# The first loads of a two-layer gated network: weights and first row in halves, other queues, fewer filler matmuls

## The chip, the core and the metric

The kernel runs on one core of a Trainium2 chip. A core has a matrix engine (TensorE, PE in the profile; its weight loads are shown apart as PEld), a vector engine (VectorE, DVE), an activation engine (ScalarE, ACT), GpSimd (POOL) and SyncE (SP), which issues transfers. ACT issues transfers too. Transfers move data from the chip's memory into the on-chip buffers and run on 16 DMA engines. The metric is the device time of one execution in microseconds (us), less being better; the time given is the median of several runs.

## The reference

x is 8 sequences of 128 tokens with 512 features, so 1024 tokens. Two layers follow one another, each a conditioning step and a gated feed-forward network with a residual:

```
base = x @ W.T                                   # 512 x 512
logits = x @ Wr.T + 5 * onehot(token id)         # 8 experts
gates = softmax over the best two logits
cond = base + 2 * sum_e gates[e] * (x @ A[e].T) @ B[e].T       # rank 16 each
x = x + down0(silu(gate0(cond)) * up0(cond))     # 4-bit weights, 1376 wide
c = x @ w1[adapter id].T                         # one matrix per sequence
x = x + down1(silu(gate1(norm(c))) * up1(norm(c)))   # 1792 wide
```

Of this the change touches the loads for the first step: `Wr` and `A` (together `WA`, 136 columns), the token ids that lie behind them, and x.

## The kernel before, in words

Features lie on the 128 partitions in 4 chunks (`KC`), tokens along the rows. Float32 products in the large matmuls are split into a high and a low part and added up in three passes (`base_products`, i = 0, 1, 2), so much of the time of ACT and VectorE goes into making these parts.

The stage at issue is the start. Here is what each line does:

- L220 loads `wa`: the expert weights `WA` and the ids, one transfer of 276 KB on SP's queue.
- L221 to L224 load x as `xb`, one transfer of 256 KB for each of the 8 sequences ("rows"). The even rows are issued by ACT, the odd ones by SP.
- L225 to L230 load W in four pieces (`wT`), B (`bT`) and a small table; all on SP. Behind them SP issues the quantised weights, their zeros and the residual.
- L243 to L246: VectorE writes a square of ones, and TensorE multiplies it by itself `NWARM` = 37 times into a bank that nobody reads.
- L287, `experts(tb)`: for each row of a half of the tokens (`tb` 0: rows 0 to 3, `tb` 1: rows 4 to 7), four accumulating matmuls over the chunks `c`, of `xb[:, row, c]` with `wa[:, c]`. A float32 matmul appears in the profile as two instructions, so a row is 8.
- L306, `gated(tb, ...)`: VectorE finds the best two experts, ACT takes one exponential (`ex`, L325) in between, VectorE weighs the low-rank products (`hg`).
- L357 to L384 make the split parts of x and of W: `x_high` and `w_high` on ACT (L359, L377), `x_scaled` on ACT (L369), `x_low`, `x_diff`, `w_low`, `w_diff` on VectorE.
- L387, `base_products`, and L414, `low_rank` (L416), add up the base and the low-rank term in PSUM; L670 and L671 (`split_condition`, on ACT and VectorE) turn the sum into the parts `a` that the first layer's gate and up matmuls (L539) read.

The order of PE, DVE and ACT in this stage is written out by hand from L697 on: `experts(0)`, the parts of rows 0 to 3, `experts(1)`, two pieces of `w_high`, `gated(0)`, the other two pieces, the parts of rows 4 to 7, and then the base products. Each engine works through its own list in that order and waits on semaphores of the others. Transfers are issued in the order of the program on each queue. PSUM tiles are pairs of banks from one pool of four.

Of the kernel before, what the change touches and what calls it, by code (L numbers as in the profile page):

```python
# [23 lines left out]
B, T, D = 8, 128, 512  # L24
NT = B * T
TB = 512
NTB = NT // TB
NWARM = 37
KC = D // P
E, R = 8, 16  # L30
LANG_BIAS = 5.0
# [57 lines left out]
def network(tc: tile.TileContext, a, out, by_groups, flag=None, again=None):  # L89


    with ExitStack() as ctx:
        network_in(ctx, tc, a, out, by_groups, flag, again)


def network_in(ctx, tc, a, out, by_groups, flag, again):
    nc = tc.nc
# [7 lines left out]
    def bank(name):  # L105
        return pair(name)[:, 0, :]
# [104 lines left out]
    xb = cp.tile([P, B, KC, T], F32, name="xb")  # L211
# [4 lines left out]
    wa_ids = cp.tile([P, KC * (E + E * R) + COND_PLACE], I32, name="wa")[:, : KC * (E + E * R) + B]  # L216
    wa = wa_ids[:, : KC * (E + E * R)].bitcast(F32).rearrange("p (c n) -> p c n", c=KC)
    ids0 = wa_ids[:, KC * (E + E * R) :]

    nc.sync.dma_start(out=wa_ids, in_=a["WA"])  # L220
    for b in range(B):  # L221
        (nc.scalar, nc.sync)[b % 2].dma_start(
            out=xb[:, b].rearrange("p c t -> p (c t)"), in_=a["xb"][b]
        )  # L224
    for m in range(KC):  # L225
        nc.sync.dma_start(out=wT[:, m, :], in_=a["WT"][:, m, :])
    nc.sync.dma_start(out=bT, in_=a["BT"])
# [16 lines left out]
    idle = bank("idle")[:, :P]  # L244
    for _ in range(NWARM):
        nc.tensor.matmul(idle, lhsT=ones, rhs=ones, start=True, stop=True)  # L246
# [1129 lines left out]
```

## Time and profile before

| what | value |
|---|---|
| median of 3 runs | 436.3 us (435.57 to 436.6) |
| the profiled execution | 436.83 us, span 434.9 us |
| mean granted clock of TensorE | 0.996 |
| base matmuls, L390, starting at | 12.90 us |
| first gate matmuls of layer 0, L539 | 43.16 us in the chain |
| `xb` on ACT's queue, 4 transfers of 256 KB | median 5.6 us from issue to landing |
| `xb` on SP's queue, 4 transfers of 256 KB | median 6.1 us |
| `wa`, 276 KB on SP's queue | 3.6 us |
| `wT`, 4 pieces of 256 KB on SP's queue | median 5.9 us |

The span runs from the first to the last instruction of the program; the execution's time also holds what lies around it. A row of the timeline has the start, the length, the engine, the line, the operation, the tiles written and read, and, in brackets, how long the engine stood idle before it and what ended that. "SPq" and "ACTq" are the sequencers that issue transfers. A busy TensorE is not TensorE at its peak, since its matmuls overlap.

### The profile page before, as it was taken

Reading aid. Unit: us, or ns where it says so; the run is one execution under the profiler, and the core shown is the slowest. Engines: PE = TensorE matmul, PEld = TensorE weight load, DVE = VectorE, ACT = ScalarE, POOL = GpSimd, SP = SyncE. Lnnn points to the kernel's source line nnn. Section 1 sums busy time; section 2 is a strip of 40 time slices with the busy share of each in tenths; the row PEclk is TensorE's granted clock in tenths of the full one; section 3 lists DMA queues with packets and bytes.
Section 4 is the critical chain, followed back from the end, with each engine's and each line's share of the span. In section 5 each row is a group of like instructions: output and inputs, shape, how many; then the busy total and the mean of one; then the engine's idle time right before and its main releaser. Section 6 shows DMA issues by size and latency. Waiting matters only on the chain.

```text
span 434.9 us, 4847 instructions
## 1 busy us (share of the span) xinstructions
PE 424.8 (98%) x1855; PEld 334.5 (77%) x1855; DVE 302.4 (70%) x432; ACT 232.0 (53%) x269; POOL 9.0 (2%) x20
## 2 busy tenths in 40 slices
PE   8999999999999999999999999999999999999992
PEld 8875778888888764447888888888888888888882
DVE  3998979998998769768179634679334676725552
ACT  5923899678877765347478132484132471425420
POOL 1000000000002001100000000000000000000000
PEclk9999999999999999999999999999999999999998
DMA  8931301010001505842114101132001110000013
GB/s 290 344 150 49 98 0 50 18 37 2 0 2 48 242 6 204 301 167 83 64 50 145 48 2 48 50 97 72 2 0 48 50 48 26 0 0 2 2 53 146
DMA packets 12094, 33.07 MB, mean 76 GB/s; under 512 B 1568, under 2 KB 4256, under 8 KB 11040
## 3 DMA queue, kind: packets, MB, share of 16 engines
q1 hardware_dynamic: 9760, 22.21, 15.3%
q0 software_dynamic: 1152, 8.39, 5.1%
q10 hardware_dynamic: 1152, 2.10, 1.3%
q8 instruction: 16, 0.26, 0.2%
q14 instruction: 14, 0.11, 0.1%
HBM read 30.59 MB, written 2.10 MB: 75 GB/s over the span
## 4 chain that ended last, share of the span: by engine, by line
PE 91%; DVE 4%; DMA 2%; ACT 1%; issue 0%; SPq 0%; ACTq 0%; DVEq 0%
PE gate L1056 18%; PE up L1056 18%; PE down L1121 17%; PE gate L539 9%; PE down L587 8%; PE up L539 8%; PE base L390 5%; PE adapt L999 5%; PE base L416 2%; DMA xb<-in_xb 2%; PE experts L293 1%; DVE xT L599 1%; PE nxT L1019 1%; ACT sl L555 1%; DVE h L558 1%; DVE w L952 1%
## 5 line engine op out<-in xcount | busy, mean ns | idle before, releaser
L1056 PE MATMUL gate<-a,w 128*128 128x512 f32 x336 | 81.8, 390 | 0.0
L1056 PE MATMUL up<-a,w 128*128 128x512 f32 x336 | 81.4, 389 | 0.0
L1121 PE MATMUL down<-h,d 128*128 128x512 f32 x336 | 76.8, 389 | 0.0
L1056 PEld LDWEIGHTS up<-a,w 128*128 128x128 f32 x336 | 63.1, 188 | 13.2
L1121 PEld LDWEIGHTS down<-h,d 128*128 128x128 f32 x336 | 63.1, 188 | 13.1
L1056 PEld LDWEIGHTS gate<-a,w 128*128 128x128 f32 x336 | 62.7, 188 | 13.5 <-ACT gate L179 0.6
L1073 DVE SCALAR_TENSOR_TENSOR h<-up,sl 128x1024 f32<-128x1024 f32 (+1 forms) x16 | 17.5, 1092 | 51.0 <-PE up L1056 44.6
L539 PE MATMUL gate<-a,dq 128*128 128x512 f32 (+1 forms) x176 | 47.7, 393 | 0.1
L539 PE MATMUL up<-a,dq 128*128 128x512 f32 (+1 forms) x176 | 47.4, 391 | 0.0
L587 PE MATMUL down<-h,wd 128*128 128x512 f32 (+1 forms) x176 | 42.3, 393 | 0.6 <-DVE h L193 0.4
L587 PEld LDWEIGHTS down<-h,wd 128*128 128x128 f32 (+1 forms) x176 | 32.5, 188 | 9.5 <-DVE h L193 0.9
L539 PEld LDWEIGHTS gate<-a,dq 128*128 128x128 f32 (+1 forms) x176 | 32.4, 185 | 8.4 <-ACT sl L555 0.6
L539 PEld LDWEIGHTS up<-a,dq 128*128 128x128 f32 (+1 forms) x176 | 32.4, 185 | 7.9 <-DVE a L671 0.3
L203 ACT ACTIVATE h<-h 128x1024 fp32r<-128x1024 f32 (+1 forms) x25 | 26.4, 1054 | 15.9 <-DVE h L1073 15.5
L1070 ACT ACTIVATE sl<-gate 128x1024 f32<-128x1024 f32 (+1 forms) x16 | 14.7, 919 | 35.8 <-PE gate L1056 35.8
L193 DVE TENSOR_TENSOR h<-h,h 128x1024 fp32r<-128x1024 f32 (+1 forms) x25 | 30.5, 1218 | 3.4 <-ACT h L203 3.4
L179 ACT ACTIVATE gate<-gate,ratio 128x1024 f32<-128x1024 f32 (+1 forms) x24 | 26.1, 1086 | 10.6 <-PE gate L539 10.6
L179 ACT ACTIVATE gate<-gate 128x1024 f32<-128x1024 f32 (+1 forms) x15 | 13.8, 923 | 30.8 <-PE gate L1056 30.8
L999 PE MATMUL adapt<-w,xT 128*128 128x512 f32 x64 | 28.9, 597 | 0.0
L179 ACT ACTIVATE down<-down 128x1024 f32<-128x1024 f32 (+1 forms) x10 | 9.2, 923 | 35.8 <-PE down L1121 35.8
L179 ACT ACTIVATE up<-up,ratio 128x1024 f32<-128x1024 f32 (+1 forms) x23 | 25.0, 1085 | 4.9 <-PE up L539 4.9
L1138 DVE SCALAR_TENSOR_TENSOR xT<-down,xT 128x1024 f32<-128x1024 f32 (+1 forms) x17 | 19.6, 1161 | 9.3 <-PE down L1121 9.1
(137 smaller groups left out, 482.6 us busy)
## 6 DMA issues: line engine op xcount, KB each, us to landing
wgu<-in_wgu SPq DMA_DIRECT2D x14, 512.0 KB, 3.3
wd<-in_wd SPq DMA_DIRECT2D x6, 512.0 KB, 3.7
qw<-in_qw_gu SPq DMA_DIRECT2D x5, 512.0 KB, 4.2
xT<-in_xT SPq DMA_DIRECT2D x2, 1024.0 KB, 11.6
xb<-in_xb ACTq DMA_DIRECT2D x4, 256.0 KB, 5.6
xb<-in_xb SPq DMA_DIRECT2D x4, 256.0 KB, 6.1
wT<-in_WT SPq DMA_DIRECT2D x4, 256.0 KB, 5.9
qwd<-in_qw_d SPq DMA_DIRECT2D x2, 512.0 KB, 8.2
```

Source lines behind the costliest of these rows:

```text
L179: nc.scalar.activation(ps, ps, AF.Copy, scale=by)
L193: nc.vector.tensor_tensor(lo, x, hi.bitcast(F32), ALU.subtract)
L203: nc.scalar.activation(hi, x, AF.Copy, scale=HSCALE)
L390: nc.tensor.matmul(base[m], lhsT=wT3[i][:, m, c * P : (c + 1) * P], rhs=x_parts(tb)[i][:, c, :], start=(i == 0 and c == 0), stop=(i == 1 a ...
L539: nc.tensor.matmul(ps, lhsT=dqs[j][:, c, half, :], rhs=a3[i][:, c, tb * TB : (tb + 1) * TB], start=(c == 0 and i == 0), stop=(i == 1), ski ...
L587: nc.tensor.matmul(ps[:, tb], lhsT=wds[k][:n, m * P : (m + 1) * P], rhs=h2[k][i][:, tb], start=(first and i == 0), stop=(i == 1), skip_gro ...
L999: nc.tensor.matmul(ps, lhsT=xT[:, c, b * T : (b + 1) * T], rhs=wt[:, c * D : (c + 1) * D], start=(c == 0), stop=(c == KC - 1),)
L1056: nc.tensor.matmul(ps, lhsT=w3[j][i][:, c, half * P : (half + 1) * P], rhs=a3[i][:, c, tb * TB : (tb + 1) * TB], start=(i == 2 and c == 0) ...
L1070: nc.scalar.activation(sl, ps, AF.Silu, scale=1.0 + EPS)
L1073: nc.vector.scalar_tensor_tensor(h, ps, 1.0 + EPS, sl, ALU.mult, ALU.mult)
L1121: nc.tensor.matmul(banks[m, tb], lhsT=d3[j][i][:, m * P : (m + 1) * P], rhs=h3[j][i][:, tb], start=(i == 0 and j == j0), stop=(j == j1 - 1 ...
L1138: nc.vector.scalar_tensor_tensor(x, ps, -EPS, x, ALU.mult, ALU.add)
```

## The change

The constant `NWARM` falls from 37 to 26. The transfer of `wa` is cut along its columns into two, each with the weights of two of the four chunks; the ids come with the second. Row 0 of x is cut into two transfers in the same way, on ACT's queue. Rows 2 and 4 stay on ACT; row 6, which was on ACT, is now on SP, behind row 5 and ahead of row 7. Rows 1, 3, 5 and 7 stay on SP. Nothing is computed differently.

```diff
-NWARM = 37
+NWARM = 26
...
-    nc.sync.dma_start(out=wa_ids, in_=a["WA"])
+    half = KC // 2 * (E + E * R)
+    for some in (slice(0, half), slice(half, None)):
+        nc.sync.dma_start(out=wa_ids[:, some], in_=a["WA"][:, some])
     for b in range(B):
-        (nc.scalar, nc.sync)[b % 2].dma_start(
-            out=xb[:, b].rearrange("p c t -> p (c t)"), in_=a["xb"][b]
-        )
+        engine = nc.scalar if b in (0, 2, 4) else nc.sync
+        n = KC * T // (2 if b == 0 else 1)
+        for i in range(0, KC * T, n):
+            engine.dma_start(
+                out=xb[:, b].rearrange("p c t -> p (c t)")[:, i : i + n], in_=a["xb"][b][:, i : i + n]
+            )
     for m in range(KC):
         nc.sync.dma_start(out=wT[:, m, :], in_=a["WT"][:, m, :])
```

## The prediction

> **What bounds the kernel now.** I read the page first, then the chain of waits in order of time, then the timeline of the first 45 us.
>
> ```profile
> PE 424.8 (98%) x1855; PEld 334.5 (77%) x1855; DVE 302.4 (70%) x432; ACT 232.0 (53%) x269; POOL 9.0 (2%) x20
> PE 91%; DVE 4%; DMA 2%; ACT 1%; issue 0%; SPq 0%; ACTq 0%; DVEq 0%
> ```
>
> TensorE is on the path for 91% of the span, so time can only be won where TensorE waits or does filler. Early on there is one such place. The chain of the first 18 us:
>
> ```profile
> 1.65 6.56 DMA xb<-in_xb
> 8.21 0.04 issue
> 8.25 4.90 PE experts L293 x40
> 13.15 3.73 PE base L390 x16
> ```
>
> Columns: start, length, what. Everything before 8.25 us hangs on one transfer: row 3 of x, second of the four rows on SP's queue, issued at 1.65 and landed at 8.21. From there to 55.24 the chain is TensorE without a break. So the question is when row 3's matmuls may start, and whether a gain there survives. The timeline of TensorE and of the engines beside it:
>
> ```profile
> 1.06 4.06 PE L246 MATMUL idle<-ones 128*128 128x128 bf16 x37 [1.06 <-DVE ones L243]
> 4.96 3.00 PE L293 MATMUL experts<-wa,xb 128*128 128x136 f32 x24
> 8.25 4.90 PE L293 MATMUL experts<-wa,xb 128*128 128x136 f32 x40 [0.29 <-DMA xb<-in_xb]
> ...
> 10.87 1.32 ACT L377 ACTIVATE wT<-wT 128x512 fp32r<-128x512 f32 x2
> 12.10 0.19 ACT L325 ACTIVATE ex<-dif 128x4 f32<-128x4 f32 x1
> ...
> 12.32 0.17 DVE L326 TENSOR_SCALAR dif<-ex 128x4 f32<-128x4 f32 x1 [0.79 <-ACT ex L325]
> ```
>
> The 37 filler matmuls start 107 ns apart and fill TensorE to 4.96. A row of x is 8 matmul instructions 116 ns apart, 0.93 us. Rows 0 to 2 occupy 4.96 to 7.80 by their starts; then TensorE stands 0.45 us until row 3 is in.
>
> **The change, part by part.** The sum is made against the profiled execution (span 434.9, its own time 436.83); the median of the runs shown is 436.3 (435.57 to 436.6). I subtract the differences from 436.3. About 0.2% (0.87 us) is what a measurement of this kernel can tell from no change.
>
> *Eleven fillers fewer.* 11 x 107 ns = 1.17 us off TensorE: the fillers end near 3.84. Alone this is worth nothing, as row 3 ends the wait. What it permits is an earlier row 0.
>
> *Halves of the weights and of row 0.* Row 0's first two of four accumulation steps need only the first halves, some 266 KB. By the stretches of one us, 26 KB came between 1 and 2 us, 276 between 2 and 3, 388 between 3 and 4: 266 KB are through near 2.9. Whole wa and row 0 were through by about 3.7 and landed at 4.3 and 4.45, some 0.7 later; the first halves so land near 3.6, the second near 4.4, as before. Row 0 runs from 3.84 and ends near 5.3 at the latest (below), not at 5.95. Rows 1 and 2 landed at 1.20 + 4.3 = 5.5 and near 5.7; the bytes ahead of them are unchanged, so row 1 starts at 5.54 in place of 5.95. **TensorE is ready for row 3 at 5.54 + 2 x 0.93 = 7.4, not at 7.8.**
>
> *Cost of halving.* One more issue on SP (0.39 to 0.43 us) puts row 1's issue at 1.65 instead of 1.20; its bytes queue behind wa until past 3, so nothing is lost; without that cover 0.45. ACT issues four transfers as before, ahead of the same table load. Packets of 1 KB for 2 KB: bounded by zero and, from the rates of later stretches with many 1 KB packets (some 350 GB/s against 390), 532 KB x that difference = 0.15 us. I take 0.1, since the first microsecond is latency anyway. The page "DMA: Bandwidth & Descriptors" of the Trainium skill, under Rules for kernel authors, says to coalesce and that transfers below 64 KB pay mostly overhead. These are 128 to 140 KB, so by the rule too the cost is part of the 0.1.
>
> *Rows 5, 6 and 7.* SP's own waits show how many transfers may be in flight:
>
> ```profile
> SPq L226 <- DMA xb<-in_xb: 2.0, 2, 1.7
> SPq L222 <- DMA xb<-in_xb: 1.9, 1, 1.9
> ```
>
> The ninth transfer (row 7) was held until 4.50, just after the first row landed; each later one likewise follows the landing of the eighth before it. With two transfers more ahead, row 5 becomes the ninth: issued near 3.6 instead of 2.13, row 6 near 4.0 instead of 2.15, row 7 near 4.5 as before, the four pieces of wT near 4.9, 5.7, 6.1, 8.4, all as before. Bytes begin about 1 us after an issue (0.74, first bytes between 1 and 2), and row 5's are due only after rows 3 and 4, past 6: no hole. TensorE wants row 5 two rows after row 3 begins, at 9.4 even if that is 7.5; it landed at 9.46 while it shared with row 6, and now goes ahead of it. What comes later on SP (bT, the small table, the quantised weights) keeps its order; its first use on VectorE at 31 us lies 10 us and more behind its landing. GpSimd's queue has no part.
>
> *When row 3 lands.* This decides, and the trace of before has only one value. Its bytes ahead (wa, rows 0 to 4) are 1.59 MB; at the measured rates they are through near 6.3 on the mean engine, and with the 0.7 of tail row 3 would land at 7.0. It landed at 8.21, so the slowest of the 16 shares trailed by 1.2. Bounds: not before 7.0 (no gain past 7.4 either) and about 8.3 (8.21 plus the 0.1 of small packets). From row 2's landing to row 3's, 2.5 us pass in which some 950 KB moved (309 to 408 KB per us), though rows 3 and 4 are 524 KB: rows 5 and 6 ran ahead on other shares. Now only row 5 can, and later. I take 7.85, nearer the row than the ideal. **Gain 0.4.**
>
> *Does the gain survive?* Row 3's start moves the first TensorE chain, but VectorE's chain from 12.32 hangs on ex, which is queued on ACT behind two conversions of wT; the second starts at 11.56, when wT's second piece has just landed (issue 5.69 + 5.8). That is bandwidth, which the change doesn't add. VectorE then has only this idle time up to the first gate matmul:
>
> ```profile
> 35.03 1.23 DVE L671 SCALAR_TENSOR_TENSOR a<-base,a 128x1024 fp32r<-128x1024 f32 x1 [0.26 <-ACT a L670]
> 36.75 1.23 DVE L671 SCALAR_TENSOR_TENSOR a<-base,a 128x1024 fp32r<-128x1024 f32 x1 [0.50 <-ACT a L670]
> ```
>
> After 36.75 it is full until past 48, and TensorE's loads there already wait for it 0.2 to 0.3 at a time. So at most 0.26 + 0.50 = 0.76 us passes through; more would be late on VectorE. 0.4 fits, less the 0.1 if wT lands later too, which the same slack takes. Afterwards everything (ACT's rescale at 54.49, the table load at 55.59) follows TensorE. **Forecast 436.3 - 0.4 = 435.9; own range 435.4 to 436.3.**
>
> **The clock: a rule against the change.**
>
> ```profile
> L246 PE MATMUL idle<-ones x37: 250/314/314, 1.1 to 4.9; 128*128 128x128 bf16 x37
> ```
>
> Minimum, median, maximum: nearly all fillers take 314 ns, the last falls to 250. The fillers ran slow and TensorE sped up near 4.9, just where they end. The profile's clock column shows 1.00 throughout and so doesn't tell it. The skill's page "TensorE: Matmul & The Clock Gate" (Part 1) says the array starts at half clock and is released after about 3.4 us of sustained work, in a window that runs free. 26 fillers are 2.8 us, too few by the rule alone. By the row, row 0's matmuls follow at 3.84 without a gap and are work too: at half speed 0.93 for the first half of row 0 (to 4.77), the second half being in by then, so TensorE is busy to past 4.9 and the release comes as before. By the row: no cost, row 0 ends by 5.3. By the rule, if the short gaps spoil a window: the rival below.
>
> **Rivals.** (1) *Row 3 is as late as before.* For it: order and bytes on each queue ahead of it are the same. It lands at 8.2 to 8.3, TensorE only waits longer: 436.3 to 436.5. Against it: the thinner traffic behind.
> (2) *Slower: the clock is released a window later.* Place: TensorE, 3.8 to 5.5. One window of 3.4 later is 8.3: row 0 ends at 5.7, row 1 at 7.55, row 2 at 8.87, row 3 starts there and not at 8.25, +0.6: 436.9. Two windows later (11.75): the eighth row ends at 15.2 instead of 12.9, +2.3: 438.6. It decides once TensorE stands idle in 3.8 to 5.5 for long, that is if the first halves land past about 4.5. Against it: the 0.45 gap before row 3 cost no clock.
> (3) *Row 3 lands early, by 7.4.* VectorE's slack is then the bound, gain 0.76: 435.5. For it: 7.0 is what the mean rate gives. Against: one share trailed even so.
> (4) *The halves are waited for as a whole,* because the tile is tracked whole: row 0 begins at 4.45, still ready for row 3 by 7.4. Same time as the forecast, so it costs no chance.
>
> **From these to the numbers.** Forecast 0.40, rival 1 0.25, rival 3 0.17, rival 2 0.18 (one window more often than two). The medians shown scatter by 0.5 to either side, so about half of rival 3 and part of the forecast's case fall below 435.4, and half and a little more of rival 2 beyond 437.2. Faster 0.25, same 0.58, slower 0.17. Low end 435.2 (rival 3 with scatter), high end 437.1 (one window late).
>
> **What would show it.** Right: fillers end near 3.8; the first experts matmul near 3.9; row 1's first near 5.5; row 3's at 7.4 to 8.0; idle before the two conversions at 35 and 36 on VectorE shrinks by the same amount; the first gate matmul is earlier by it. Wrong: row 3 lands at 8.2 or later; row 1 lands past 5.6 (the halves cost more on SP than taken); experts matmuls more than 116 ns apart after 5 us (the clock); idle time on VectorE at 35 and 36 gone with TensorE waiting at 43.

## The result and the profile after: slower by 0.3%

The changed kernel takes 437.49 us in the median of 22 runs (436.38 to 440.59), the kernel before 436.58 in 22 (435.57 to 437.62). The ratio is 1.0032, 95% interval 1.0018 to 1.0046: some 1.4 us slower, where 0.4 faster was forecast. (The medians lie 0.9 apart; the means lie 1.4 apart, as in the ratio, for the slowest times pull. Below, too, the ratio can differ from that of the medians.) Two things stand out already. The fastest run is only 0.8 over the fastest of before, but the slowest is 3 over its slowest: the times scatter over 4 us in place of 2.

The profiled execution took 437.63 us, span 435.8. Its chain of waits up to 18 us (start, length, what) answers to the one shown of before:

```profile
1.65 5.80 DMA xb<-in_xb
7.45 0.04 issue
7.49 6.75 PE experts L300 x56
14.24 3.72 PE base L397 x16
```

The rows run unbroken from 7.49 instead of 8.25, but now 56 instructions are left instead of 40: seven rows, not five. The transfer that releases them is **row 1**, landed at 7.45; before, it was there at 5.50. The experts end at 14.24 instead of 13.15. The timeline of TensorE:

```profile
1.07 2.96 PE L253 MATMUL idle<-ones 128*128 128x128 bf16 x26 [1.07 <-DVE ones L250]
3.81 1.22 PE L300 MATMUL experts<-wa,xb 128*128 128x136 f32 x4
5.43 0.73 PE L300 MATMUL experts<-wa,xb 128*128 128x136 f32 x4 [0.39 <-DMA xb<-in_xb]
7.49 6.75 PE L300 MATMUL experts<-wa,xb 128*128 128x136 f32 x56 [1.33 <-DMA xb<-in_xb]
```

The first half of row 0 starts at 3.81, as forecast. Then come two holes: one to 5.43 for the second half of row 0, which landed at 5.38 and not 4.4 (in the traces of three kernels below with the same halves it landed at 4.3), and one to 7.49 for row 1. ACT shows a second lateness:

```profile
11.44 0.63 ACT L384 ACTIVATE wT<-wT 128x512 fp32r<-128x512 f32 x1
12.86 0.63 ACT L384 ACTIVATE wT<-wT 128x512 fp32r<-128x512 f32 x1 [0.80 <-DMA wT<-in_WT]
13.40 0.19 ACT L332 ACTIVATE ex<-dif 128x4 f32<-128x4 f32 x1
```

The second piece of wT was issued at 8.04, just after row 2 had landed (8.02), and ex comes 1.3 later than before. So TensorE is 1.1 late and VectorE 1.3, and the slack between them takes the difference: of the two idle times on VectorE the first is gone, the second stays.

```profile
36.10 1.22 DVE L678 SCALAR_TENSOR_TENSOR a<-base,a 128x1024 fp32r<-128x1024 f32 x1
37.82 1.23 DVE L678 SCALAR_TENSOR_TENSOR a<-base,a 128x1024 fp32r<-128x1024 f32 x1 [0.50 <-ACT a L677]
```

The first gate matmul stands at 44.23 in the chain instead of 43.16 (+1.07), and the span is 0.8 longer. In between, VectorE runs up to 1.6 later than before: the stretches behind the change add and take back several tenths in a single execution, so spans of single profiles can't be compared that finely. Nor does one profile explain times up to 440.

### The profile page after: what moved, and what is told of

The parts are those of the page before. It is cut to its first block, busy times and chain, and to the rows that moved or that the text cites. A ratio compares the mean times of both kernels' runs of the same rounds, so it can differ in the third digit from the quotient of the medians.

```text
span 435.8 us, 4829 instructions
## 1 busy us (share of the span) xinstructions
PE 424.3 (97%) x1844; PEld 333.9 (77%) x1844; DVE 302.3 (69%) x432; ACT 232.3 (53%) x269; POOL 9.5 (2%) x20
## 4 chain that ended last, share of the span: by engine, by line
PE 92%; DVE 3%; DMA 2%; ACT 2%; issue 0%; SPq 0%; ACTq 0%; DVEq 0%
PE gate L1063 18%; PE up L1063 17%; PE down L1128 17%; PE gate L546 9%; PE up L546 8%; PE down L594 8%; PE base L397 5%; PE adapt L1006 5%; PE base L423 2%; PE experts L300 2%; DMA xb<-in_xb 1%; DMA wgu<-in_wgu 1%; PE nxT L1026 1%; ACT sl L562 1%; DVE h L565 1%; DVE w L959 1%
```

## The experiments: one part at a time

Two theories. **T**: the halves make row 1's transfer late. **C**: with 26 fillers TensorE's clock is released late in some executions. Each of the first four kernels has one part or two; all times are against the kernel before, run on the same chip.

**Fillers alone** (transfers of before):

```diff
-NWARM = 37
+NWARM = 26
```

> Only the filler count changes (26 for 37); the transfers are those of before. Theory T (transfers: the halves put row 1's data third on SP's queue, where the first packets are slow, and row 1 lands near 7.4 instead of 5.5): no part of it is here, so the time equals before within 0.3 us, row 1 lands near 5.5, row 3 near 8.2. Theory C (clock: too little filler, TensorE's release to full speed comes a window later in some executions): median 0.5 to 1 us slower than before and single times up to 440, as in the changed kernel.

438.06 us (435.98 to 439.42) against 436.4; ratio 1.0031, 1.0019 to 1.0043. Theory C, and dearer than it said. The transfers landed as before (row 1 at 5.53, row 3 at 7.98). Timeline of TensorE, and then its experts matmuls by stretches of one us (start and end, length, busy and number, clock, share of DMA, GB/s):

```profile
1.06 2.95 PE L246 MATMUL idle<-ones 128*128 128x128 bf16 x26 [1.06 <-DVE ones L243]
4.53 9.54 PE L293 MATMUL experts<-wa,xb 128*128 128x136 f32 x64 [0.52 <-DMA xb<-in_xb]
```

```profile
5.00:6.00 1.00, 1.00 (x6) 1.00 0.95 287
6.00:7.00 1.00, 1.00 (x7) 1.00 1.03 371
7.00:8.00 1.00, 1.00 (x6) 1.00 1.06 367
8.00:9.00 1.00, 1.00 (x9) 1.00 1.02 295
9.00:10.00 1.00, 1.00 (x11) 1.00 1.03 256
```

Six matmuls per us until 8, eleven from 9 on: TensorE ran at half rate to near 8.4, busy all the while. (The clock column says 1.00 throughout; it tells nothing here, the count does.) The fillers end near 3.8 and row 0 starts at 4.53: a hole of 0.5 to 0.7 us. Before, the fillers reached to row 0 without one, and the release came near 4.9. The Trainium skill's page "TensorE: Matmul & The Clock Gate" (Part 1) says that the release follows a window of about 3.4 us of sustained work, and that these windows run free of the kernel; the clock records further down agree.

**Loads alone** (the changed kernel, `NWARM` 37 again):

> The changed kernel with 37 fillers again; all its transfers stay. Theory T: row 1 lands near 7.4, TensorE starts its unbroken run there, the median is about 0.9 us over before. Theory C: the release comes near 4.9 again, median within 0.3 us of before and the scatter as narrow as before's (2 us).

436.77 us (435.65 to 438.47) against 436.4; ratio 1.0013, 1.0005 to 1.0021. Theory T, at 0.6 us and not 0.9: row 1 landed at 7.41.

```profile
4.99 1.75 PE L300 MATMUL experts<-wa,xb 128*128 128x136 f32 x8
7.45 6.75 PE L300 MATMUL experts<-wa,xb 128*128 128x136 f32 x56 [0.71 <-DMA xb<-in_xb]
```

Row 0 starts at 4.99 and is done well before row 1 is there, though at half rate: its eight instructions take 1.75 us, and the release came at 6.2 and not 4.9. The scatter is back to 2.8 us, nearer to before's. Part of the 0.6 may be the clock's too, as the hole before row 1 (0.71) is longer than the one in the kernel with fillers alone; no trace of this kernel shows a late release.

**Row 6 on SP alone**:

```diff
-        (nc.scalar, nc.sync)[b % 2].dma_start(
+        (nc.scalar if b in (0, 2, 4) else nc.sync).dma_start(
```

> Only row 6 moves from ACT's queue to SP's; no halves, 37 fillers. Theory T and theory C both: no change (within 0.3 us), row 3 lands near 8.2. If the queue of rows 5 to 7 is what costs (wT's second piece landing later, VectorE late), it shows here: wT's second piece past 12, median up to 1 us slower.

436.72 us; ratio 1.0005, 0.9997 to 1.0014: no difference within that interval, though wT's second piece landed at 12.02. Row 3 landed at 7.49 and not near 8.2. Its timeline shows the free-running window from the other side:

```profile
1.07 3.73 PE L246 MATMUL idle<-ones 128*128 128x128 bf16 x37 [1.07 <-DVE ones L243]
4.63 7.80 PE L293 MATMUL experts<-wa,xb 128*128 128x136 f32 x64
```

The same 37 fillers took 3.73 us, not 4.06: here the release came near 4.2, within them. The fillers and their start are those of before, and nothing else ran on TensorE by then, so this is a matter of the execution and not of the kernel.

**Halves alone** (rows on their queues of before, `NWARM` 37):

> Only the halves of the weights and of row 0; rows on their queues of before, 37 fillers. Theory T: row 1 lands near 7.4 and the median is about 0.9 us over before. If the queues are the cost and not the halves: within 0.3 us of before, with row 1 near 5.5. Theory C: within 0.3 us.

437.25 us; ratio 1.0017, 1.001 to 1.0025. Row 1 landed at 7.11. So the halves are the slow part of the loads; for the queue of row 6 no cost is seen.

**Fillers in the hole** (the changed kernel, and after row 0):

```diff
+            if tb == 0 and b == 0:
+                for _ in range(20):
+                    nc.tensor.matmul(idle, lhsT=ones, rhs=ones, start=True, stop=True)
```

> The changed kernel with 20 more fillers between row 0 and row 1, where TensorE waits for row 1 (about 5.9 to 7.4); transfers as in the changed kernel, row 1 late as there. Clock theory (a window of about 3.4 us in which TensorE stood idle for a fifth or more doesn't release it, and then rows run at half speed): the scatter closes, no single time past 438.6, median near that of the loads with 37 fillers, 436.8. If the scatter comes from the transfers: median stays near 437.5 to 438 with single times to 440.

436.90 us (435.96 to 437.51); ratio 1.0009, 1.0 to 1.0018. The scatter closes to 1.6 us, as theory C has it, with row 1 as late as before (7.25). The fillers stand here:

```profile
3.81 1.60 PE L300 MATMUL experts<-wa,xb 128*128 128x136 f32 x8
5.25 1.28 PE L309 MATMUL idle<-ones 128*128 128x128 bf16 x20
7.29 6.75 PE L300 MATMUL experts<-wa,xb 128*128 128x136 f32 x56 [0.76 <-DMA xb<-in_xb]
```

Of the changed kernel's 1.4 us, about 1.0 goes by giving TensorE filler to do. The 0.4 left is near the cost of the loads alone. (The two intervals just touch, so the 1.0 is rough, and a hole of 0.76 remains.)

**Eight fillers** (before, `NWARM` 8), the dose carried further:

> Before with 8 fillers instead of 37 (they end near 1.9, row 0 starts near 4.5); transfers as before. Clock theory: no window can be filled before the rows begin, so the release falls between 7.9 and 11.4 us in every execution and each row before it takes 1.85 us instead of 0.93; the experts end at 13.6 to 15.4 instead of 13.15: median about 1.5 us over before, no single time below 436.4. If the fillers' end and not the window counted (26 lost it by chance of its gap), the median is that of 26 fillers or less, with fast single times as well.

438.54 us (437.12 to 439.03) against 436.83. No single time reaches before's median, as expected. (The ratio over rounds is 1.0032, 1.0018 to 1.0046.) Experts matmuls by stretches:

```profile
8.00:9.00 1.00, 1.00 (x7) 1.00 1.00 277
9.00:10.00 1.00, 1.00 (x6) 1.00 0.94 262
10.00:11.00 1.00, 1.00 (x10) 1.00 1.02 332
```

Half rate to near 10.2. Rows at half rate are work too, and in time they earn the release; but it costs 0.93 us for each row done before it, less what TensorE would have waited for row 3 anyway. In the ratio, 8 fillers cost no more than 26 (1.0031). What differs is the spread: no fast time is left.

**When the clock was released.** Each trace also records when the granted clock changes. The first record is the release; nothing is recorded before it, and the column of the stretches fills that with 1.00. Near the end of the program the clock is recorded as falling to 0.5, in ten of the 14 traces 125 times 3.413 us after the release and in four 124 times. So the changes lie on a grid of 3.413 us, which fits the window of about 3.4 us named above. With the grid laid back from each release, one sees how long TensorE stood idle in the window that ended with the release, and in those before it:

| kernel | release, us | idle in its window, us | idle in earlier windows (their end) |
|---|---|---|---|
| row 6 on SP alone | 4.23 | 0.25 | |
| before | 4.93 | 0.00 | |
| changed | 5.17 | 0.14 | |
| loads alone | 6.21 | 0.00 | |
| row 0 in halves only (below) | 6.76 | 0.00 | 1.13 (3.34) |
| fillers alone | 8.36 | 0.00 | 0.52 (4.95) |
| eight fillers | 10.18 | 0.00 | 1.14 (6.76), 2.38 (3.35) |
| row 1 between the halves (below) | 10.44 | 0.24 | 0.82 (7.02), 0.87 (3.61) |

The column of earlier windows leaves out those that began more than 0.1 us ahead of the program. In the six traces not listed the release came between 4.74 and 5.55 with 0.03 us idle or less. Up to 0.25 us idle in a window the release came; with 0.52 and more it did not. That the changed kernel's trace shows an early release was luck: its window ended at 5.17, and the first hole began at 5.03.

**Which transfer is late?** Four kernels move the places on the queues, all with 37 fillers. The first cuts only row 0 in halves, the second only wa; the third puts the small table first on SP; the fourth has SP's order first half of wa, row 1, second half of wa.

> Only row 0 comes in halves (ACT's queue), wa whole, 37 fillers, queues of before. Theory P (the third transfer of a queue is the slow one, whichever data it has): on SP row 1 is again second and lands near 5.5, row 3 third, past 7.4; on ACT row 2 is third and lands past 7 instead of 5.7, so rows run unbroken from row 2 at the earliest: about 0.3 us slower than before. Theory B (bytes ahead count, not places): all landings as before within 0.3 us.

> Only the weights wa come in halves (SP's queue), row 0 whole, 37 fillers, queues of before. Theory P (the third transfer of a queue is late): row 1 lands near 7 instead of 5.5 and TensorE runs unbroken from there, about 0.5 to 0.7 us over before. If it takes the halves on both queues: row 1 lands before 6 and the time is before's within 0.3 us.

> Before, with the small table (78 KB) moved from behind bT to the front of SP's queue; 37 fillers, nothing halved. Theory P: row 1 is now third on SP and lands near 7 instead of 5.5; about 0.7 us slower. Theory B: row 1 lands 0.2 us later than before, near 5.7; no change in the time.

> The changed kernel with 37 fillers and SP's queue in the order first half of wa, row 1, second half of wa, row 3. Theory P: row 1, now second, lands near 5, the second half of wa, now third, past 6.5, though it is half the size; TensorE waits for it in row 0 and then runs unbroken. Theory B: the second half of wa lands near 4.7, row 1 near 4.5, and the time is that of before.

Landings on SP's queue in us, each from the issue and its time to landing in that kernel's trace (the first row is the kernel before, which the ratios are against):

| kernel | first | second | third | time, ratio (interval) |
|---|---|---|---|---|
| before | wa 4.3 | row 1 5.5 | row 3 8.2 | 1 |
| fillers alone | wa 4.3 | row 1 5.5 | row 3 8.0 | 1.0031 |
| changed | half wa 3.4 | half wa 4.05 | **row 1 7.45** | 1.0032 |
| loads alone | half wa 3.4 | half wa 4.1 | **row 1 7.4** | 1.0013 |
| halves alone | half wa 3.45 | half wa 4.1 | **row 1 7.1** | 1.0017 |
| wa in halves only | half wa 3.8 | half wa 4.9 | **row 1 7.8** | 1.0028 (1.0017 to 1.0039) |
| row 0 in halves only | wa 4.1 | row 1 5.0 | row 3 7.3 | 1.002 (1.0011 to 1.0029) |
| row 1 between the halves | half wa 3.6 | row 1 4.65 | **half wa 7.1** | 1.0033 (1.002 to 1.0047) |
| small table first | table 3.8 | wa 5.1 | row 1 6.4 | 1.0006 (0.9997 to 1.0014) |

In eight of these nine traces the third transfer lands 2.3 to 3.4 us after the second, whichever data it has and even at half size; first and second lie 0.6 to 1.3 apart. In the five traces not listed the third lands 2.0 to 3.1 after the second. The clearest is row 1 between the halves. TensorE there waits for 140 KB of weights:

```profile
4.99 1.22 PE L305 MATMUL experts<-wa,xb 128*128 128x136 f32 x4
7.26 8.73 PE L305 MATMUL experts<-wa,xb 128*128 128x136 f32 x60 [1.06 <-DMA wa<-in_WA]
```

Its time is not the transfer's alone: behind the hole, and with all 37 fillers, TensorE ran at half rate to 10.4, as the count of experts matmuls shows.

```profile
8.00:9.00 1.00, 1.00 (x7) 1.00 1.05 406
9.00:10.00 1.00, 1.00 (x6) 1.00 1.15 356
11.00:12.00 1.00, 1.00 (x11) 1.00 0.75 256
```

With row 0 alone in halves it is ACT's third, row 2, that comes last (8.20), and six rows then run from 8.25. The exception is the small table first: there the third, row 1, followed the second by only 1.3, and rows ran unbroken from 5.22. So the place is not the whole of it. The traces' records of single packets show how the third is late: a few packets trail. In row 1 between the halves, 121 of the 128 packets of the second half of wa had begun by 5.33 and the last four began at 6.32 to 6.70; the two slowest took 0.72 and 1.47 us, most 49 ns. In the changed kernel eight packets of 2 KB on SP's queue, begun between 3.49 and 4.19, took 0.67 to 1.88 us, against a median of 84 ns. What holds them back (what the queue keeps ready, the sizes ahead of them, the memory) was not found, and of each kernel there is one trace.

**Two attempts at a better version.** Before, with row 3 issued by GpSimd; and the same with ex moved on ACT ahead of the second conversion of wT:

```diff
-        (nc.scalar, nc.sync)[b % 2].dma_start(
+        (nc.gpsimd if b == 3 else (nc.scalar, nc.sync)[b % 2]).dma_start(
...
-            for m in range(2):
-                w_high(m)
+            w_high(0)
             hg0 = gated(0, rows_of(exp0))
-            for m in range(2, KC):
+            for m in range(1, KC):
                 w_high(m)
```

> Before with row 3 issued by GpSimd, the first transfer of a queue of its own; all else as before, 37 fillers. Theory P: row 3 is no longer third on SP and lands before 7, rows run unbroken from row 0 or 1, base matmuls start near 12.4 instead of 12.9, and the time falls by up to 0.5 us (VectorE's slack bounds it at 0.76). Theory B (bytes ahead decide): row 3 takes its share from rows 0 to 2, which land later, and nothing is won; up to 0.5 us slower if row 0 comes past 5.2.

> Row 3 issued by GpSimd as in the run before, and on ACT the exponential ex moved ahead of the second conversion of wT; 37 fillers, nothing halved. If VectorE's chain from ex is what holds the first layer's start once row 3 is early: ex comes near 11.6 instead of 12.1 to 12.3, VectorE goes on 0.5 us earlier, the first gate matmul starts near 42.4 instead of 43.2, and the time is 0.4 to 0.7 us below before. If another wait binds first (the second piece of wT for the base matmuls, TensorE's own rows): within 0.2 us of before.

436.64 us, ratio 0.9997 (0.999 to 1.0004), and 436.84, ratio 1.0003 (0.9995 to 1.0012): neither differs from before, though the intervals leave room for gains of 0.4 and 0.2 us. Row 3 landed at 7.28 and 7.09, and the rows ran unbroken:

```profile
4.99 7.79 PE L293 MATMUL experts<-wa,xb 128*128 128x136 f32 x64
```

(Row 3 on GpSimd.) With ex moved it started at 11.73 instead of 12.10 only, as the first conversion of wT waited for its piece until 11.19. In the two profiles the first gate matmul stands at 42.79 and 42.72, up to 0.4 before that of before; the times don't show it. No version tried is shown to beat the kernel before.

## Why the prediction was wrong, step by step

- **Fillers end near 3.8 and row 0 begins there: right** (3.81).
- **"The bytes ahead of them are unchanged, so row 1 starts at 5.54": wrong, the first step that failed.** Row 1 started at 7.49. Bytes ahead alone don't set the landing: behind two short transfers row 1 landed at 7.1 to 7.8 in all five kernels that have them, against 5.0 to 5.6 where wa and row 1 are first and second. The profile of before held a sign: row 3, third, landed 2.7 after row 1, second. I read that as the tail of one slow share, which fits the trailing packets, but put it on row 3, and took the cost of the halves for packets and issues, 0.1 us. It is about 0.6 (loads alone: 0.0013 of 436.4; interval 0.2 to 0.9). Why the third transfer's packets trail stays open.
- **"By the row: no cost" for the clock: wrong, and the larger term.** I let the row (the last filler speeding up near 4.9) outweigh the rule, on the ground that row 0's matmuls follow without a gap. In the changed kernel's profile that held, and rows from 5.4 on ran at full rate. But one profile shows one position of a window that runs free: the release came anywhere from 4.2 to 6.8 where fillers and rows left no hole. Nor did row 0 follow without a gap where it came whole: with fillers alone and the transfers of before, a gap of 0.5 to 0.7 us was left, TensorE stayed at half rate to 8.4, and the cost was 1.35 us (0.0031 of 436.4). In the changed kernel, the holes before row 0's second half and before row 1 can play the part of the gap; filling the second brought back about 1.0. That its slow times are late releases is inferred from this and from the other kernels' traces, as no slow execution of it was traced. Rival 2 had the mechanism, at 0.18, and its 2.3 for two windows, with the 0.6 of the loads, reaches to 439.5 from before's median and 440.5 from before's slowest time; the slowest was 440.59. It should have been the forecast for the fillers.
- **The two costs overlap.** 1.35 and 0.6 would be 1.9; together they are 1.4. That a row waiting for its data is not also slowed fits this; it was not measured by itself.
- **wT's pieces "near 4.9, 5.7, ... as before": wrong.** The first was issued at 5.77, behind row 7 (5.40, just after the second half of row 0), and the second at 8.04, just after row 2. The rule of the eighth transfer was one off: in both traces some issues wait for the landing of the seventh before, as row 7 did at 4.50 for row 0 (4.49), not for wa (4.32). By itself this need not cost time: with row 6 alone moved, the second piece landed 0.5 later than before and no cost was seen.
- **Row 3 would land at 7.85 and decide: moot.** It landed at 8.70 and nobody waited for it. Nor is one value enough: with the transfers of before it landed at 8.21 (37 fillers), 7.98 (26) and 7.46 (8), so it varies by more than the 0.36 that was to be won. The sum of bytes was a little off as well: by the rates of before 1.39 MB have come by 6.0, so 1.59 MB are through near 6.5 and not 6.3, and the early bound is 7.2 and not 7.0.
- **At most 0.76 passes VectorE: not tested,** as no first gate matmul came early enough; the two attempts gave at most 0.4 in the profile, row 6 alone moved 0.7 (42.42).

## What to carry to other kernels

A filler that holds the clock has to reach to the first real matmul, and real work with holes in it isn't a substitute: judge it over many executions, since the window lies differently in each, and look at matmuls per microsecond, not at one profile's clock column. Before cutting a first transfer in two, look, on this evidence, at which transfer now becomes the third of its queue and who waits for it: the first half came 0.9 us sooner here and row 1 two us later. Where single times scatter more after a change, the change has touched something that varies with the execution, and the median of three runs won't tell how much.

## What the runs showed that was not expected

The release of the clock came anywhere between 4.2 and 10.4 us, in kernels whose fillers all began at 1.06 or 1.07. With 26 fillers TensorE worked at half rate from 4.5 to 8.4 without a break before it was released, and the window before had 0.52 us of idleness in it; and 37 fillers did not bring an early release where a hole of 1.06 us came soon after them (row 1 between the halves, 10.4). And a 140 KB transfer issued at 1.65 landed at 7.1 while 256 KB issued before it on the same queue at 1.20 landed at 4.65. First and second on SP's queue, half transfers landed sooner than whole ones (3.4 against 4.3, 4.1 against 5.5); third, half size was no help.
